# Attention loop of a transformer block: bias adds of the residual rows, the three parts of the normalisation, and the start of the output projection moved to other steps

## The chip, the core and the metric

The kernel runs on one core of a Trainium2 chip. A core has a matrix engine (PE), a vector engine (DVE), an activation engine (ACT), a general engine (POOL) and a queue for transfers (SP); each takes its instructions strictly in the order in which the program issues them, and waits on semaphores for the others. POOL issues transfers too. The metric is the device time of one launch in microseconds (us).

## The reference

One block: attention with low-rank updates on its four projections, a residual sum, a layer normalisation, then a mixture of experts with a shared expert, a residual sum and a second layer normalisation. All data is float32; x is 2 x 1024 x 512, 16 heads of 32.

```python
def lora_linear(x, W, b, Bm, Am):
    out = jnp.einsum('bld,od->blo', x, W) + b
    upd = jnp.einsum('blr,or->blo', jnp.einsum('bld,rd->blr', x, Bm), Am)
    return out + SCALING * upd
...
scores = jnp.einsum('bhqd,bhkd->bhqk', q, k) * SCALE
attn = jax.nn.softmax(scores, axis=-1)
out = jnp.einsum('bhqk,bhkd->bhqd', attn, v)
...
x = _layernorm(x + attention(x), axis=-1)
x = _layernorm(x + moe(x), axis=-1)
```

## The kernel before, in words

The change lies in the attention loop (lines 617 to 855); the projections ahead of it and the experts behind it are as they were.

The work of attention is cut into 16 units (`NU`): a unit is one group of four heads, of one batch, against 512 query rows. Eight groups with two query halves each make the 16. A unit is cut into eight steps, one for each block of 128 keys, so there are 128 steps (`NS`), t = 0 to 127; unit u is t // 8 and step k of it is t % 8. The texts call them "unit 13, step 3". Each step has four slots, one for each head.

A step (`st_step`, line 629) issues for each of its four heads one matmul of transposed scores into a PSUM bank (`st`, line 638) and one exponential on ACT into half of a tile `pt` (line 647). The banks for `st` come from a pool of three (`one`). After the exponential of slot q the functions in `between[q]` are issued, so their place in that list is their place in the order of every engine. Around the steps stand these:

- `maxima`: the scores of a unit are computed twice. The first time, 12 steps ahead (`LEAD`), only the row maxima are wanted: `s1_step` (line 196) does a matmul into one of four banks `s1` (line 203) and a maximum on DVE (line 211). `S_AT` says how many come in each slot, 32 in a unit. After the last of a unit, `finish_max` (line 219) transposes the maxima on PE (into a bank of `one`), splits them into a high and a low part on ACT and DVE (`mh`, `ml`, lines 224 and 225) and sends them by DMA into two extra rows of the query tile, so that the second computation of the scores subtracts them. The last unit's is issued by the loop itself.
- `av_step`: every second step, in slot 3, eight groups of matmuls of the probabilities with the values (line 657).
- `adds` (line 673): the softmax's sums are first added up over key blocks. In a usual unit POOL issues two accumulating transfers after step 2 and two after step 3 (`pt` onto `pt`, line 682), and then eight adds of 128x1024 (line 685), two after each of steps 4 to 7.
- `finish` (line 692): the matmuls with ones that end the sums (line 698), in slot 1 of step 4 of the next unit, a copy on ACT, and a round trip through memory that spreads the 2048 sums over 128 partitions; `invert` (line 719) takes their reciprocals on DVE in step 6 and sends them back as `rb`.
- `normalize` (line 732), in three parts, two units after the unit it belongs to: part 0 multiplies the attention output by the reciprocals (DVE, line 738), part 1 casts the result to its high part (ACT, line 743), part 2 subtracts for the low part (DVE, line 745). Table `NRM` gives for each part (units later, step, slot).
- `load_res` and `add_res` (lines 747 and 752): the 16 blocks of 128 residual rows are loaded into `x1a` and `x1b` at the steps of `RES_AT`, and POOL adds the output projection's bias to them at the steps of `RES_ADDS`, one instruction of 128x512 each.
- `oproj` (line 759): the output projection of one block of rows, 12 matmuls; for the first batch eight blocks, at the steps of `OPROJ_AT`, four matmuls in each of slots 0 to 2. Behind each come, on DVE, the sum with the residual row and the statistics, one step later two small instructions on POOL (`norm_root`) and four steps later the scaling on ACT. It reads what `normalize` left for units 0 to 7.

Within a slot the order is: the maxima that come first, `av_step`, `finish`, the maxima that come second, `adds`, the parts of `normalize`, `invert`, `add_res`, and the projection. The order is written out by hand with these tables; nothing reorders it (`manual_schedule` for all five engines).

In the kernel before, parts 0 and 1 are issued in slot 0 of step 3 and part 2 in slot 2 of step 3. The bias adds stand in steps 9, 13, 25, 29, 41, 45, 57, 61, 73, 77, 89, 93, 103, 105, 114 and 115: up to step 93 that is steps 1 and 5 of the odd units.

Of the kernel before, what the change touches and what calls it, by code (L numbers as in the profile page):

```python
# [20 lines left out]
NU = 16  # L21
# [11 lines left out]
LEAD = 12  # L33
LATE, OP_ONE = (0,), 0
NS = NU * 8
# [19 lines left out]
AVQ = 3  # L55
# [2 lines left out]
FIN = {None: (1, 4, 1), NU - 3: (1, 3, 1), NU - 2: (1, 2, 3)}  # L58
REC = {None: (1, 6, 3), NU - 3: (1, 5, 1)}
NRM = {  # L60
    None: ((2, 3, 0), (2, 3, 0), (2, 3, 2)),
    NU - 3: ((1, 7, 3), (1, 7, 3), (1, 7, 3)),
    NU - 2: ((1, 4, 1), (1, 4, 1), (1, 4, 1)),
}
# [13 lines left out]
    NU - 2: {1: "bb1 dd01", 3: "dd23 vv4", 4: "vv5", 5: "vv6", 6: "vv3 vv7"},  # L78
    NU - 1: {1: "bb1 dd01", 3: "dd23 vv4", 4: "vv5", 6: "vv3"},
}  # L80
OPROJ_AT = (68, 70, 72, 74, 76, 78, 80, 82)
RES_AT = tuple(8 * i + (2 if i % 2 else 6) for i in range(8)) + (70, 74, 86, 90, 100, 102, 106, 110)
RES_ADDS = tuple(t + 3 for t in RES_AT[:14]) + (114, 115)
RB = 2
BTB = 4
AHEAD = 5
# [26 lines left out]
def kernel(  # L113
# [5 lines left out]
    def f(ap):  # L119
        return ap.bitcast(F32)  # L120
# [42 lines left out]
    def load_k(g, cs=slice(0, 1024), hs=slice(0, 4)):  # L163
        kt = Ks[g % 2]
        for blk, hl in ((0, 0), (1, 1), (2, 0)):
            sp.dma_start(
                out=f(kt[32 * blk : 32 * blk + 32, hs, cs]),
                in_=qk_d[1, g // NG, g % NG, hl].rearrange("(h p) t -> p h t", p=32)[:, hs, cs],
            )

    def load_v(g):
        if g < NG:
            vts[g] = x1b[:, :, g * P : g * P + P]
        else:
            vts[g] = mp_.tile([P, 8, P], F32, name=f"vt{g}", tag="vt", bufs=2)
        sp.dma_start(
            out=vts[g],
            in_=v_d[g // NG].rearrange("(c p) d -> p c d", p=P)[
                :, :, (g % NG) * P : (g % NG) * P + P
            ],  # L180
        )

    def load_q(u, hs=slice(0, 4)):
        g, qb = u // 2, u % 2
        for blk, hl in ((0, 0), (1, 0), (2, 1)):
            sp.dma_start(
                out=f(Qs[u % 3][32 * blk : 32 * blk + 32, hs]),
                in_=qk_d[0, g // NG, g % NG, hl].rearrange("(h p) t -> p h t", p=32)[
                    :, hs, qb * 512 : qb * 512 + 512
                ],  # L190
            )
# [27 lines left out]
    def finish_max(u):  # L219
        mp = one.tile([P, 512], F32, name=f"mp{u}", tag="one")  # L220
        pe.transpose(mp[0:16, 0:P], mts[u], ident)
        mh = mp_.tile([16, P], F32R, name=f"mh{u}", tag="mh", bufs=2)
        ml = mp_.tile([16, P], F32R, name=f"ml{u}", tag="ml", bufs=2)
        act.copy(mh, mp[0:16, 0:P])
        dve.tensor_tensor(ml, mp[0:16, 0:P], f(mh), ALU.subtract)
        for i, m_ in enumerate((mh, ml)):
            sp.dma_start(
                out=f(Qs[u % 3][96 + i : 97 + i, :, :]).rearrange(
                    "o h (q t) -> o (h q) t", t=P
                ),  # L230
                in_=f(m_),
            )
# [386 lines left out]
    with ph2, tc.manual_schedule(engines={mybir.EngineType.PE}):  # L619
# [31 lines left out]
        def av_step(t):  # L651
            u, kc = t // 8, t % 8
            g = u // 2
            if kc == 0:
                avs[u] = avp.tile([P, 512], F32, name=f"av{u}", tag="av")
            for h in range(4):
                pe.matmul(  # L657
                    avs[u][32 * h : 32 * h + 32, :],
                    vts[g][:, kc, 32 * h : 32 * h + 32],
                    pts[t, h // 2][:, h % 2, :],  # L660
                    start=kc == 0,
                    stop=kc == 7,
                    skip_group_check=True,
                )
# [4 lines left out]
        def av_out(u):  # L669
            raws[u] = ap.tile([P, 512], F32, name=f"ae{u}", tag="ae", bufs=2)  # L670
            act.copy(raws[u], avs[u])
# [20 lines left out]
        def finish(u):  # L692
            sm = one.tile([P, 512], F32, name=f"sm{u}", tag="one")
            parts = [lambda h, k_=k_: pts[u * 8 + k_, h // 2][:, h % 2, :] for k_ in direct(u)]
            parts.append(lambda h: accs[u, h // 2][:, h % 2, :])
            for i, pf in enumerate(parts):
                for h in range(4):
                    pe.matmul(
                        sm[32 * h : 32 * h + 32, :],
                        ones32,  # L700
                        pf(h),
                        start=i == 0,
                        stop=i == len(parts) - 1,
                        skip_group_check=True,
                    )
            if u >= RDIR:
                rc = ap.tile([P, 512], F32, name=f"rc{u}", tag="rc", bufs=1)
                dve.reciprocal(rc, sm)
                fin[u] = rc
                return  # L710
            rc = ap.tile([P, 512], F32, name=f"rc{u}", tag="rc", bufs=1)
            act.copy(rc, sm)
            sd = dram.tile([4, 512], F32, name=f"sd{u}")
            sp.dma_start(out=sd, in_=rc[0:P:32, :])
            r16 = ap.tile([P, 16], F32, name=f"r16_{u}", tag="r16", bufs=1)
            sp.dma_start(out=r16, in_=sd.rearrange("h (j c) -> (h j) c", c=16))
            fin[u] = r16
# [29 lines left out]
        def load_res(n):  # L747
            b, i = divmod(n, 8)
            r0 = b * L + i * P
            sp.dma_start(out=x1[b][:, i, 0:D], in_=x[r0 : r0 + P, :])  # L750

        def add_res(n):
            b, i = divmod(n, 8)
            pool.tensor_tensor(x1[b][:, i, 0:D], x1[b][:, i, 0:D], bo_bc, ALU.add)
# [29 lines left out]
        def run(gen):  # L784
            for _ in gen:
                pass
# [12 lines left out]
        def at_step(table, t, q):  # L799
            for v in range(max(t // 8 - 2, 0), t // 8):  # L800
                at = table.get(v, table[None])
                at = at[q] if isinstance(at[0], tuple) else at
                if (v + at[0]) * 8 + at[1] == t:
                    yield v

        for t in range(NS):
            u, k = t // 8, t % 8
            if k == 0:

                if u % 2 == 0 and 2 <= u and u // 2 + 1 < B * NG:  # L810
                    for hs in (slice(0, 2), slice(2, 4)):
                        load_k(u // 2 + 1, hs=hs)
                        load_q(u + 2, hs)
                elif u >= 1 and u + 2 < NU:
                    load_q(u + 2)
                if u % 2 and NG <= u // 2 + 1 < B * NG:
                    load_v(u // 2 + 1)
            if t in RES_AT:
                load_res(RES_AT.index(t))
            between = [[], [], [], []]  # L820
            for q in range(4):
                between[q] += [maxima] * S_AT[k][q][0]
            if t + LEAD == NS + 1:
                between[0].append(lambda: finish_max(NU - 1))

            if t and t % 2 == 0:
                between[AVQ].append(lambda: (av_step(t - 2), av_step(t - 1)))
                if k == 0:
                    between[AVQ].append(lambda: av_out(u - 1))
            for v in at_step(FIN, t, 0):  # L830
                between[FIN.get(v, FIN[None])[2]].append(lambda v=v: finish(v))
            for q in range(4):
                between[q] += [maxima] * S_AT[k][q][1]
            if t:
                between[AVQ].append(lambda: adds(t - 1))
            for q in range(3):
                for v in at_step(NRM, t, q):
                    between[NRM.get(v, NRM[None])[q][2]].append(lambda v=v, q=q: normalize(v, (q,)))
            for v in at_step(REC, t, 0):
                if v < RDIR:  # L840
                    between[REC.get(v, REC[None])[2]].append(lambda v=v: invert(v))
            if t in RES_ADDS:
                between[3].append(lambda: add_res(RES_ADDS.index(t)))

            if t in OPROJ_AT:
                op0 = oproj(0, OPROJ_AT.index(t), OPER)
                for q in range(3):
                    between[q].append(lambda q=q, op0=op0: run(op0) if q == 2 else next(op0))
            st_step(t, between)
            for _, fn in [x for x in later if x[0] == 0]:  # L850
                fn()
            later[:] = [(n - 1, fn) for n, fn in later if n]
            if t - NS >= OPROJ1:
                next(op10, None)
# [349 lines left out]
    for st, (blk, nb) in enumerate(BLOCKS):  # L1204
        hss = []
        for c in range(6):
# [22 lines left out]
            for v in range(c * nb, c * nb + nb):  # L1229
                bv, cv = blk + v // 6, v % 6  # L1230
                n = (bv - NB + 1) * 6 + cv
# [10 lines left out]
    with tc.manual_schedule(engines=MAN4):  # L1242
        last = None
        for e in range(E):
            nxt = e + 1
            hss = []
            for c in range(6):
# [4 lines left out]
                n = nxt * 6 + c  # L1252
# [113 lines left out]
```

## Time and profile before

| | |
|---|---|
| median of 3 runs | 1041.44 us (1038.62 to 1042.34) |
| the profiled execution's own time | 1041.44 us |
| its span, first to last instruction | 1039.7 us |
| mean granted clock of PE | 0.992 |
| PE, DVE, ACT, POOL busy | 1007.0, 684.1, 527.8, 535.0 us |
| attention loop (first to last `st` matmul) | 156.4 to 592.5 us of the span |
| bias add, line 754 | 16 times, 1087 to 1937 ns |
| part 0, line 738 (on `rb`) | 14 times, 680 to 4325 ns, median 1190 |
| part 2, line 745 | 15 times, 673 to 821 ns |

Times in the profile are from the span's start. A line of the timeline gives start, duration, engine, source line, operation, what is written and read by the program's names, and how many instructions are merged; in brackets stands how long the engine was idle before and who released it. Lines of groups give busy time and mean duration of one, and then the idle time ahead of them. `L754` is line 754 of the kernel.

### The profile page before, as it was taken

To read this page: it belongs to the slowest core of one execution; us is meant where nothing else is said; L and a number is where in the kernel's file an instruction comes from. 1 tells how busy PE (TensorE), PEld (TensorE's weight loads), DVE (VectorE), ACT (ScalarE), POOL (GpSimd) and SP (SyncE) were. 2 spreads that over 40 slices of the span, in tenths; PEclk is the share of its full clock that TensorE was granted. 3 is DMA by queue.
4 is the path that set the end of the run, shared out by engine and by line. 5 is a ranking of instruction groups with operands and counts; after the bars stand their busy time and mean duration, and the time that the engine had idled before them with its cause. 6 is when DMAs were issued, how large, how long until landed. Compare 5 with 4: busy or idle time off the path is not lost. (4 is left out here: it accounts for less than half of the span.)

```text
span 1039.7 us, 15687 instructions
## 1 busy us (share of the span) xinstructions
PE 1007.0 (97%) x5606; PEld 728.0 (70%) x5606; DVE 684.1 (66%) x1156; ACT 527.8 (51%) x1000; POOL 535.0 (51%) x404
## 2 busy tenths in 40 slices
PE   8999999999999999999989999999999999999994
PEld 6888885555545555655544489888787899999994
DVE  6743788788888887788878773232253467777752
ACT  5322216666767665576657835122122366555662
POOL 5000005989898977869887164000015055666774
PEclk9999999999999999999989999999999999999998
DMA  9866875586868784667964631000009567777621
GB/s 277 289 230 214 245 222 114 126 190 138 190 134 194 154 193 95 127 138 151 197 153 85 151 112 62 22 21 11 31 30 302 177 205 233 258 244 254 222 82 61
DMA packets 87374, 164.75 MB, mean 158 GB/s; under 512 B 15944, under 2 KB 24648, under 8 KB 87296
## 3 DMA queue, kind: packets, MB, share of 16 engines
q1 hardware_dynamic: 74240, 117.59, 38.9%
q0 software_dynamic: 13056, 46.16, 19.9%
q8 instruction: 44, 0.72, 0.3%
q14 instruction: 34, 0.28, 0.1%
HBM read 96.10 MB, written 33.80 MB: 125 GB/s over the span
## 5 line engine op out<-in xcount | busy, mean ns | idle before, releaser
L211 DVE TENSOR_REDUCE mt<-s 128x1 f32<-128x512 f32 x512 | 317.8, 680 | 69.1 <-PE s L203 68.8
L647 ACT ACTIVATE pt<-st 128x512 f32<-128x512 f32 x512 | 266.6, 611 | 113.7 <-PE st L638 107.1
L685 POOL TENSOR_TENSOR pt<-pt,pt 128x1024 f32<-128x1024 f32 x112 | 264.3, 2389 | 37.1 <-ACT pt L647 18.6
L638 PE MATMUL st<-qs,ks 98*128 98x512 f32 x512 | 197.7, 417 | 11.1 <-ACT pt L647 8.8
L203 PE MATMUL s<-ks,qs 96*128 96x512 f32 x512 | 186.8, 403 | 0.2
L638 PEld LDWEIGHTS st<-qs,ks 98*128 98x128 f32 x512 | 92.8, 189 | 94.5 <-ACT pt L647 37.9
L682 POOL DMA_DIRECT2D pt<-pt x64 | 56.2, 1004 | 185.6 <-issue 144.6
L931 PE MATMUL h<-xthe,w13s 128*128 128x256 f32 x704 | 130.0, 283 | 0.0
L203 PEld LDWEIGHTS s<-ks,qs 96*128 96x128 f32 x512 | 97.3, 190 | 36.2 <-DVE mt L211 10.8
L931 PEld LDWEIGHTS h<-xthe,w13s 128*128 128x128 f32 x704 | 110.7, 191 | 0.4
L919 POOL TENSOR_TENSOR w2s<-w2r,w2s 128x512 fp32r<-128x512 f32 x42 | 65.9, 1590 | 68.2 <-ACT w2s L918 65.3
L931 PE MATMUL h<-xtle,w13s 128*128 128x256 f32 x352 | 100.3, 285 | 0.4 <-DVE xtle L484 0.4
L1121 POOL DMA_INDIRECT xd_d<-x1a,slot_i x8 | 7.9, 984 | 139.3 <-DVE slot_i L1118 137.2
L931 PEld LDWEIGHTS h<-xtle,w13s 128*128 128x128 f32 x352 | 67.4, 191 | 1.5 <-DVE xtle L484 0.8
L657 PE MATMUL av<-pt,vt 128*32 128x512 f32 x512 | 62.3, 598 | 0.0
L657 PE MATMUL av<-pt,x1b 128*32 128x512 f32 x512 | 61.6, 598 | 0.0
L1017 PE MATMUL y<-w2s,hs 128*128 128x512 f32 x260 | 60.9, 390 | 0.0
L1017 PEld LDWEIGHTS y<-w2s,hs 128*128 128x128 f32 x260 | 48.2, 188 | 10.2 <-DVE hs L999 0.5
L342 ACT ACTIVATE oh<-o,bqk_sb 128x512 fp32r<-128x512 f32 x32 | 22.0, 690 | 56.2 <-PE o L327 52.5
L586 DVE TENSOR_TENSOR w13s<-x1a,w13s 128x1024 fp32r<-128x1024 f32 x32 | 46.7, 1460 | 4.6 <-issue 4.1
L327 PE MATMUL o<-xh,wh 128*128 128x512 f32 x116 | 45.5, 392 | 1.0 <-DVE ol L343 1.0
L327 PE MATMUL o<-xl,wh 128*128 128x512 f32 x116 | 45.3, 391 | 0.0
(571 smaller groups left out, 1704.2 us busy)
## 6 DMA issues: line engine op xcount, KB each, us to landing
pt<-pt POOLq DMA_DIRECT2D x64, 512.0 KB
x1a<-in_w_dram SPq DMA_DIRECT2D x32, 512.0 KB
w2r<-in_w_dram SPq DMA_DIRECT2D x42, 256.0 KB
ks<-qkd SPq DMA_DIRECT2D x36, 256.0 KB
qkd<-oh SPq DMA_DIRECT2D x32, 256.0 KB
qkd<-ol SPq DMA_DIRECT2D x32, 256.0 KB
qs<-qkd SPq DMA_DIRECT2D x30, 256.0 KB
qs<-qkd SPq DMA_DIRECT2D x36, 128.0 KB
```

What stands on the lines that cost most here:

```text
L203: pe.matmul(s1, Qs[u % 3][0:96, h, qt * P : qt * P + P], Ks[g % 2][0:96, h, kh * 512 : kh * 512 + 512], start=True, stop=True,)
L211: dve.tensor_reduce(mts[u][:, c, kh : kh + 1], s1, AX.X, ALU.max)
L327: pe.matmul(o, lhs, rhs, start=k + i == 0, stop=k + i == KC + 1)
L586: (pool if e < 0 else dve).tensor_tensor(lo, raw, f(hi), ALU.subtract)
L638: pe.matmul(sb, Ks[g % 2][:, h, kc * P : kc * P + P], Qs[u % 3][:, h, :], start=True, stop=True,)
L647: act.activation(pts[t, h // 2][:, h % 2, :], sb, AF.Exp, scale=SCALE)
L657: pe.matmul(avs[u][32 * h : 32 * h + 32, :], vts[g][:, kc, 32 * h : 32 * h + 32], pts[t, h // 2][:, h % 2, :], start=kc == 0, stop=kc == 7 ...
L682: pool.dma_start(out=pts[to, pr], in_=pts[i, pr], accum_op=ALU.add)
L685: eng.tensor_tensor(accs[u, pr], accs[u, pr], pts[i, pr], ALU.add)
L919: pool.tensor_tensor(hl[:, 1, :], raw, f(hl[:, 0, :]), ALU.subtract)
L931: pe.matmul(hp[:, j * 256 : j * 256 + 256], lhs, rhs[:, k, :], start=n == 0, stop=n == 11,)
L1017: pe.matmul(o, lhs, rhs, start=n == 0, stop=n == 16)
```

## The change

Four things are moved; no arithmetic is added or taken away.

- The bias adds go to slot 3 of step 3 of each unit from 1 to 13, one in each and two in unit 13 (steps 11, 19, ..., 107, 107), and the last two stay in steps 114 and 115. The lookup allows two in one step.
- Part 0 of the normalisation goes from slot 0 to slot 1 of step 3, part 1 from slot 0 to slot 3 of step 3, part 2 from slot 2 of step 3 to slot 1 of step 4. The special rows of `NRM` are as before.
- The output projection of the first batch starts in step 70 and ends in step 84, two steps later.
- `finish_max` of the last unit goes from the start of slot 0 in step 117 to slot 3 of step 116, behind `av_step`.

```diff
 NRM = {
-    None: ((2, 3, 0), (2, 3, 0), (2, 3, 2)),
+    None: ((2, 3, 1), (2, 3, 3), (2, 4, 1)),
     NU - 3: ((1, 7, 3), (1, 7, 3), (1, 7, 3)),
     NU - 2: ((1, 4, 1), (1, 4, 1), (1, 4, 1)),
 }
...
-OPROJ_AT = (68, 70, 72, 74, 76, 78, 80, 82)
+OPROJ_AT = (70, 72, 74, 76, 78, 80, 82, 84)
 RES_AT = tuple(8 * i + (2 if i % 2 else 6) for i in range(8)) + (70, 74, 86, 90, 100, 102, 106, 110)
-RES_ADDS = tuple(t + 3 for t in RES_AT[:14]) + (114, 115)
+RES_ADDS = tuple(range(11, 108, 8)) + (107, 114, 115)
...
                 between[q] += [maxima] * S_AT[k][q][0]
-            if t + LEAD == NS + 1:
-                between[0].append(lambda: finish_max(NU - 1))
 
             if t and t % 2 == 0:
                 between[AVQ].append(lambda: (av_step(t - 2), av_step(t - 1)))
                 if k == 0:
                     between[AVQ].append(lambda: av_out(u - 1))
+            if t + LEAD == NS:
+                between[AVQ].append(lambda: finish_max(NU - 1))
...
-            if t in RES_ADDS:
-                between[3].append(lambda: add_res(RES_ADDS.index(t)))
+            for n, at in enumerate(RES_ADDS):
+                if at == t:
+                    between[3].append(lambda n=n: add_res(n))
```

## The prediction

> **What bounds the kernel now.** The page's first part, then the waits of each engine in the attention stretch (150 to 600 us), then the timeline there. Columns of the first line: busy us (share of the span) x instructions.
>
> ```profile
> PE 1007.0 (97%) x5606; PEld 728.0 (70%) x5606; DVE 684.1 (66%) x1156; ACT 527.8 (51%) x1000; POOL 535.0 (51%) x404
> ```
>
> PE is the bound, so only what lets PE issue sooner counts. The change touches the attention loop alone. In its groups (busy us, mean ns of one | idle before, releaser) one row is odd:
>
> ```profile
> L685 POOL TENSOR_TENSOR pt<-pt,pt 128x1024 f32<-128x1024 f32 x112 | 264.3, 2389 | 37.1 <-ACT pt L647 18.6 <-DMA pt<-pt 15.5 <-ACT mh L224 1.2
> L738 DVE TENSOR_TENSOR ae<-ae,rb 128x512 f32<-128x512 f32 x14 | 22.7, 1620 | 0.5 <-DMA rb<-rd 0.4
> L745 DVE TENSOR_TENSOR at_l<-ae,at_h 128x512 fp32r<-128x512 f32 x15 | 10.3, 689 | 0.1
> L754 POOL TENSOR_TENSOR x1a<-x1a,bo_bc 128x512 f32<-128x512 f32 x8 | 9.6, 1194 | 0.0
> ```
>
> L738 (part 0 of the normalisation) and L745 (part 2) are the same work, yet part 0 takes 1620 ns on average. The timeline of unit 13 says why (start us, us, instructions; in brackets the idle time before and its releaser):
>
> ```profile
> 527.47 4.33 DVE L738 TENSOR_TENSOR ae<-ae,rb 128x512 f32<-128x512 f32 x1
> ...
> 528.88 2.37 POOL L754 TENSOR_TENSOR x1b<-x1b,bo_bc 128x512 f32<-128x512 f32 x2
> ...
> 531.15 1.72 POOL L682 DMA_DIRECT2D pt<-pt  x2
> ...
> 531.83 0.62 ACT L743 CAST at_h<-ae 128x512 fp32r<-128x512 f32 x1 [2.25 <-DVE ae L738]
> ...
> 532.99 0.80 PE L638 MATMUL st<-qs,ks 98*128 98x512 f32 x1 [2.63 <-ACT pt L647]
> ```
>
> Part 0 (DVE, to 531.79) ends 0.55 us after the last of POOL's consecutive adds (531.24): DVE stood through the end of L685's add and both L754. ACT's cast (part 1) waits for it ahead of the next exponentials, and PE waits for a score buffer. In unit 3 it is the same on a small scale: part 0 from 241.26 to 243.29, POOL's L754 until 242.74. Where POOL issues DMAs instead (L682), L745 takes 673 to 681 ns.
>
> The wait of 2.63 us also cost clock. The windows show the granted clock at 1.00, then 0.83, 0.50, 0.50, 0.81 (530 to 540 us); shorter waits in units 5 and 11 (1.40 and 1.25) did not.
>
> **How much there is.** From the first score matmul of a step to that of the next, in the timeline: unit 1, which normalises nothing, has 1.97 us in step 3 and 6.68 in step 4, together 8.65. Units 2, 4, 6, 8 (without its projection) and 12 take 9.05; units 3, 5, 7, 11, 13 take 9.55, 10.33, 9.52, 10.20, 14.38. Units 9 and 10 lose 0.22 each in step 3. Over the floor: 5 x 0.40 + (0.90 + 1.68 + 0.87 + 1.55 + 5.73) + 0.44 = 13.2 us. The odd units stand out because the bias adds of steps 1 and 5 fall in odd units only, and that of step 1 is POOL's last work before part 0.
>
> **The change, part by part.**
>
> *Bias adds (POOL, 16 x 1.1 to 1.3 us, as many as before).* They now stand behind the four DMA issues of steps 2 and 3. POOL is free there: it issues four in about 3.5 us (0.87 each) and then waits for the first landing, which lets the next add start 4.55 to 4.67 us after the first issue in units 3, 5, 7, 11 (0.64 us idle in unit 3) and 6.0 to 7.6 in units 2, 4, 6, 8, 12, where key loads are in front. The loads (L750, SP) don't move; each row is loaded at least five steps before its add.
>
> *Part 0, one slot later, behind two score maxima.* DVE reaches it about 2.2 us into step 3 (unit 1: maxima at 1.00 and 1.61). POOL then issues DMAs in every unit, so it takes 0.68. Part 1 goes behind the fourth exponential; the sum's 16 matmuls (1.85 us) cover its 0.61. Gain: the 13.2. Not all stays: exponentials of units 5 and 13 also wait for POOL's last add of the unit before (0.26 and 0.70 us on ACT); with steps shortened I keep 0.3 and 0.6. Units 2 and 12 wait for the landing of the sums (DVE 1.41 and 1.72 us at L722), and starting earlier doesn't bring that forward: 0.8 given back.
>
> *Part 2, step 3 slot 2 to step 4 slot 1.* This is the dangerous one. It leaves POOL's DMA stretch and goes behind the maximum that follows the sum's matmuls. In unit 1 that starts 5.39 us after the start of step 3; with part 0 ahead 5.5, so part 2 comes up at 6.1. In the odd units POOL has by then issued its DMAs (to 3.8 or 4.0), added the bias (to about 5.0) and started the first add of step 4 (5.0 to 7.4); the second follows (7.4 to 9.7). In even units the first add starts 6.56 (unit 8) to 8.46 (unit 12) after step 3, so part 2 is ahead by 0.5 or more: nothing lost.
>
> When does part 2 finish in an odd unit? If DVE gets in between the two adds: 7.4 + 0.55 = 7.95. If only after both: 9.7 + 0.55 = 10.25. PE's next need is the second score matmul of step 5, at 8.65 + 0.25 = 8.9, whose buffer is freed by `ml` (L225), which stands one maximum (0.60) and 0.27 behind part 2: part 2 must end by 8.0. So the stall is 0 or some 2.3 to 2.4 us; the maxima that free PE's `s` banks queue behind part 2 likewise.
>
> Which? In this trace the second add starts late: 0.12 to 0.23 us after the first ends (units 2, 3), because its DMA lands 2.5 us after the first DMA and an add lasts 2.38. With the bias add in front the first add starts up to 0.3 later, and that gap closes. At boundaries without a gap DVE was passed over each time: in units 3, 5, 7, 11 once each and in unit 13 twice. I take "after both" for units 3, 7, 11 (3 x 2.4 = 7.2), "between" for unit 5, where the DMAs start later and the gap stays (1.0, as it ends late), the ends being 0 and 2.4 for each.
>
> The Trainium skill, "SBUF — State Buffer", section "Who interferes with whom", says that a VectorE instruction with two SBUF inputs and a GpSimd one that reads SBUF exclude each other, the first to issue holding the port for one whole instruction. Read so, a waiting DVE would enter at the next boundary: L738 in unit 13 would have taken 2.05 us, not 4.33, and the sum below would be 7.2 us and its clock loss lower. The rows decide against that reading.
>
> Unit 13 has two bias adds in step 3 (steps 103 and 105 become 107). POOL is late there anyway (last add of unit 12 ended 0.97 into step 3): DMAs to 4.9, adds to 7.3, then two adds without gap to 12.0. Part 2 ends at 12.6 against a need of about 8.5: 4.1 lost, plus the clock. Half clock cost this unit 9.36 - 6.80 = 2.56 in step 4; the same again: 6.7.
>
> Clock in units 3, 7, 11: waits of 2.3 us lie between 1.40 (none) and 2.63 (a drop); nearer the upper, so I count a drop in one and a half of three: 3.9, ends 0 and 7.8. The Trainium skill, "TensorE: Matmul & The Clock Gate", section "What's actually happening", puts the return to half rate after an idle window of about 3.4 us; by it these units would lose none of this, but the trace shows a drop with 2.63.
>
> *Last maximum transpose (`finish_max(15)`), one slot earlier.* PE waits 0.82 us at 573.92 for `qs<-ml`. `ml` now stands ahead of DVE's adds of that step (2.36 us) and its DMA goes out some 1.3 us earlier: -0.8; the adds behind it are 0.3 later and have slack (0.4 us idle before the next L738). Ends -0.8 and +0.5.
>
> *Output projection, two steps later.* The same 96 matmuls, still two of eight steps that also carry a sum (68 and 76 become 76 and 84). Behind each row DVE's 0.69 + 0.70 + 0.18 + 0.15, POOL's 0.64 + 0.27 and ACT's 0.82 move along. In units 8 to 10 the steps are 2.8 us longer and POOL idles in them; counted 0. Without that cover, POOL's 8 x 0.9 = 7.2 would queue before the adds.
>
> **Sum**, against the profiled execution's own 1041.44 us (span 1039.7), which is also the median: -13.2 + 0.9 + 0.8 + 7.2 + 1.0 + 6.7 + 3.9 - 0.8 = +6.5, so 1048 us.
>
> **Rivals.**
> 1. *DVE enters between the two adds in all of units 3, 5, 7, 11.* For: the gap of 0.12 to 0.23 us today. Against: the bias add eats it. -13.2 + 0.9 + 0.8 - 0.8 + 1.6 + 6.7 = -4.0: 1037.
> 2. *It enters in unit 13 too*, ending about 10.4 instead of 12.6, without the clock drop (2.0 for 6.7): -8.7: 1033, faster, decided by whether a waiting DVE wins a boundary where POOL's next add is ready.
> 3. *Even units lose too*, if their first add starts before 6.1: five times 2.4 and half a clock drop (1.3), +18: 1066. Against: their landing follows the key loads, which don't move.
>
> **Numbers.** Forecast 0.45, own range 1043 to 1053; rival 1: 0.28; rival 2: 0.17; rival 3: 0.10. A measurement of this kernel tells some 0.5% (5.2 us) from no change. Faster by more: rival 2 and a third of rival 1, 0.27. Slower by more: rival 3 and most of the forecast, 0.43. Range 1032 to 1057, from rival 2 to the forecast with every clock drop.
>
> **What would show it.** L738 at 680 to 700 in all units: step right. L745's mean far over 689, its long ones (3 to 6 us) in odd units ending 0.55 after an L685 add: forecast. L745 at about 2 us there: rival 1. Granted clock below 1.00 in the slices of units 3 to 13: the clock term. No wait for `qs<-ml` near 574: the transpose. Wrong altogether if L745 isn't held at all, or if POOL's adds fall so late that exponentials wait for their `pt` buffers.

## The result, and the profile after

The changed kernel takes 1042.95 us (median of 22 runs, 1041.64 to 1044.21); the kernel before, on the same chip, 1039.80 us (22 runs, 1036.17 to 1043.12). The ratio is 1.0033, 95% interval 1.0023 to 1.0044: slower by 0.33%, some 3.4 us. The direction is that of the forecast, the size half of it, and 0.33% lies below the half per cent that the prediction took as its bound for "no change".

The profiled execution of the changed kernel took 1042.95 us, with a span of 1041.2. First the page's first part (busy us, share of the span, instructions), then the groups of the attention stretch, 150 to 610 us:

```profile
PE 1010.9 (97%) x5606; PEld 727.4 (70%) x5606; DVE 688.0 (66%) x1156; ACT 531.7 (51%) x1000; POOL 538.0 (52%) x404
```

```profile
L685 POOL TENSOR_TENSOR pt<-pt,pt 128x1024 f32<-128x1024 f32 x112 | 266.6, 2420 | 21.2 <-ACT pt L647 10.8 <-DMA pt<-pt 8.4 <-ACT mh L224 1.2
L745 DVE TENSOR_TENSOR at_l<-ae,at_h 128x512 fp32r<-128x512 f32 x15 | 27.5, 1836 | 0.1
L754 POOL TENSOR_TENSOR x1a<-x1a,bo_bc 128x512 f32<-128x512 f32 x8 | 14.7, 1838 | 0.0
L738 DVE TENSOR_TENSOR ae<-ae,rb 128x512 f32<-128x512 f32 x14 | 10.3, 735 | 0.0
```

Parts 0 and 2 have changed places. Part 0 (L738) fell from 22.7 to 10.3 us in all; part 2 (L745) rose from 10.3 to 27.5. POOL's adds (L685) take nearly what they took, 2420 for 2389 ns on average. (L754 is recorded longer because its record now begins while the transfer ahead of it is still being issued: in unit 3 the issue is recorded until 244.52 and the bias add from 243.87.)

The long L745 of unit 13, in the timeline of that unit:

```profile
530.49 2.86 POOL L754 TENSOR_TENSOR x1b<-x1b,bo_bc 128x512 f32<-128x512 f32 x2
532.79 7.47 POOL L685 TENSOR_TENSOR pt<-pt,pt 128x1024 f32<-128x1024 f32 x3
532.88 7.94 DVE L745 TENSOR_TENSOR at_l<-ae,at_h 128x512 fp32r<-128x512 f32 x1
541.48 1.58 PE L203 MATMUL s<-ks,qs 96*128 96x512 f32 x2 [5.21 <-DVE mt L211]
...
545.12 7.07 POOL L685 TENSOR_TENSOR pt<-pt,pt 128x1024 f32<-128x1024 f32 x3 [4.86 <-ACT pt L647]
```

DVE stands from 532.88 to 540.82, through the end of the second bias add and three adds of L685, and ends 0.56 us after the third has ended (540.26). POOL paused there because its fourth add waited for exponentials (4.86 us, the last line), and these for PE, which the waiting DVE held up. The maxima behind part 2 (L211) free PE's `s` banks, so PE waits 5.21 us. What that cost in clock shows in the windows (us; then PE, PEld, DVE, ACT, POOL busy and number, granted clock, DMA share, GB/s):

```profile
538.50:541.00 2.50, 0.00 (x0) 0.00 (x0) 2.50 (x2) 0.00 (x0) 1.76 (x1) 0.88 0.25 44
541.00:543.50 2.50, 2.02 (x4) 1.33 (x5) 2.50 (x6) 0.00 (x0) 0.00 (x0) 0.50 0.10 9
543.50:546.00 2.50, 2.50 (x7) 1.92 (x7) 2.50 (x5) 1.79 (x3) 0.89 (x1) 0.50 0.34 99
```

PE gets half clock while it catches up: 541.00 to 546.00 in these rows.

Unit 3 stands for the odd units without a second bias add. Its timeline:

```profile
243.87 1.95 POOL L754 TENSOR_TENSOR x1a<-x1a,bo_bc 128x512 f32<-128x512 f32 x1
245.65 2.51 POOL L685 TENSOR_TENSOR pt<-pt,pt 128x1024 f32<-128x1024 f32 x1
...
248.22 5.08 POOL L685 TENSOR_TENSOR pt<-pt,pt 128x1024 f32<-128x1024 f32 x2
```

```profile
246.37 2.34 DVE L745 TENSOR_TENSOR at_l<-ae,at_h 128x512 fp32r<-128x512 f32 x1
250.16 0.50 PE L203 MATMUL s<-ks,qs 96*128 96x512 f32 x1 [0.19 <-DVE mt L211]
```

Here DVE comes in after one add: that add ends at 248.16, L745 at 248.72. The second add's record begins at 248.22, 0.06 us after the first has ended. It could not begin sooner, since it waits for its transfer, whose landing the trace puts at 248.08. In unit 13 that transfer had landed at 534.58, 1.09 us before the add ahead of it ended (535.67), so POOL did not pause.

The units by the timeline, from the first score matmul of one to that of the next (us):

| unit | 2 | 3 | 5 | 7 | 8 to 10 | 11 | 12 | 13 | 14 | 0 to 14 |
|---|---|---|---|---|---|---|---|---|---|---|
| before | 25.86 | 26.91 | 27.13 | 26.35 | 101.18 | 27.03 | 25.87 | 31.74 | 24.03 | 417.48 |
| after | 25.45 | 27.21 | 26.97 | 26.85 | 101.02 | 27.83 | 25.47 | 34.64 | 25.85 | 421.86 |

The loop's units 0 to 14 are 4.4 us longer. The stretches before and behind, where the two kernels issue the same work, were 2.9 us shorter in this execution (156.43 to 155.33 and 465.82 to 464.03), so the two profiled executions differ by only 1.5.

### The profile page after: what moved, and what is told of

Same layout as the page of the kernel before. It is cut to its first block, busy times and chain, and to the rows that moved or that the text cites. A ratio compares the mean times of both kernels' runs of the same rounds, so it can differ in the third digit from the quotient of the medians.

```text
span 1041.2 us, 15685 instructions
## 1 busy us (share of the span) xinstructions
PE 1010.9 (97%) x5606; PEld 727.4 (70%) x5606; DVE 688.0 (66%) x1156; ACT 531.7 (51%) x1000; POOL 538.0 (52%) x404
## 5 line engine op out<-in xcount | busy, mean ns | idle before, releaser
L211 DVE TENSOR_REDUCE mt<-s 128x1 f32<-128x512 f32 x512 | 318.3, 680 | 68.8 <-PE s L203 68.6
L647 ACT ACTIVATE pt<-st 128x512 f32<-128x512 f32 x512 | 269.6, 609 | 122.1 <-PE st L638 115.0
L685 POOL TENSOR_TENSOR pt<-pt,pt 128x1024 f32<-128x1024 f32 x112 | 266.6, 2420 | 21.2 <-ACT pt L647 10.8
L203 PE MATMUL s<-ks,qs 96*128 96x512 f32 x512 | 193.0, 413 | 6.5 <-DVE mt L211 6.0
L580 ACT CAST w13s<-x1a 128x1024 fp32r<-128x1024 f32 x32 | 33.4, 1045 | 24.7 <-DMA x1a<-in_w_dram 18.5
```

The lines of the kernel that those rows point to most:

```text
L203: pe.matmul(s1, Qs[u % 3][0:96, h, qt * P : qt * P + P], Ks[g % 2][0:96, h, kh * 512 : kh * 512 + 512], start=True, stop=True,)
L211: dve.tensor_reduce(mts[u][:, c, kh : kh + 1], s1, AX.X, ALU.max)
L647: act.activation(pts[t, h // 2][:, h % 2, :], sb, AF.Exp, scale=SCALE)
L685: eng.tensor_tensor(accs[u, pr], accs[u, pr], pts[i, pr], ALU.add)
```

## The experiments

**My theory after the result:** the bias adds in step 3 and part 2 in step 4 are each good or harmless alone, and only together put a DVE instruction that needs POOL to stand still right behind a bias add, inside POOL's adds. Rivals: moving the parts is what costs, whatever POOL does; the change to the output projection costs; unit 13 alone, with its two bias adds, decides.

### The bias adds alone

```diff
-RES_ADDS = tuple(t + 3 for t in RES_AT[:14]) + (114, 115)
+RES_ADDS = tuple(range(11, 108, 8)) + (107, 114, 115)
```

(on the kernel before, with the lookup that allows two in one step)

> Bias adds in step 3 as in the change; normalisation, projection and last transpose as before. Theory (the loss is part 2 standing behind POOL's adds): part 2 stays in POOL's DMA stretch, so L745 at 0.68 in every unit; L738 no longer has a bias add in front and is at most 1.2 us; units 3, 5, 7, 11, 13 fall to the length of the even ones: 0.5 + 1.3 + 0.5 + 1.2 + 5.3, so 8 to 9 us faster than before (ratio 0.991 to 0.993). Rival (the bias adds in step 3 hold up POOL's own adds and through them the loop): slower than before by 2 us or more.

Measured: 1030.86 us, ratio 0.9903 (0.9870 to 0.9937). The groups of its attention stretch:

```profile
L738 DVE TENSOR_TENSOR ae<-ae,rb 128x512 f32<-128x512 f32 x14 | 12.9, 921 | 0.7 <-DMA rb<-rd 0.6
L745 DVE TENSOR_TENSOR at_l<-ae,at_h 128x512 fp32r<-128x512 f32 x15 | 10.4, 692 | 0.1
```

The whole gained a little more than expected. Part 2 is short in every unit of the loop's general row; part 0 is short too but for units 3, 5 and 13, where it still takes 1.68, 1.65 and 2.04 us behind POOL's last add, more than the 1.2 expected. Unit 13, in the timeline:

```profile
526.86 1.83 POOL L682 DMA_DIRECT2D pt<-pt  x2 [0.34 <-ACT pt L647]
527.14 0.68 DVE L745 TENSOR_TENSOR at_l<-ae,at_h 128x512 fp32r<-128x512 f32 x1
528.39 2.65 POOL L754 TENSOR_TENSOR x1b<-x1b,bo_bc 128x512 f32<-128x512 f32 x2
530.69 5.02 POOL L685 TENSOR_TENSOR pt<-pt,pt 128x1024 f32<-128x1024 f32 x2
```

Part 2 ran while POOL issued transfers, and the same two bias adds and the same L685 stand behind it, with nobody waiting for POOL. Unit 13 takes 26.77 us, against 31.74 before and 34.64 after. This one line of the change gives 1%.

### The three parts and the projection alone

```diff
-    None: ((2, 3, 0), (2, 3, 0), (2, 3, 2)),
+    None: ((2, 3, 1), (2, 3, 3), (2, 4, 1)),
...
-OPROJ_AT = (68, 70, 72, 74, 76, 78, 80, 82)
+OPROJ_AT = (70, 72, 74, 76, 78, 80, 82, 84)
```

> The three parts of the normalisation and the projection as in the change, bias adds and last transpose as before. Theory: L738 0.68 everywhere; L745 some 2.3 us in units 3, 5, 7, 11, which stay 0.3 shorter to 0.8 longer than before; unit 13 has its bias adds ahead of the DMAs again, its first add lands later than part 2, so L745 is 0.7 there and the unit loses its 7 us: 2 to 5 us faster than before (ratio 0.995 to 0.998). Rival (bias adds are the cause): 9 us faster or more, with no long L745.

Measured: 1035.61 us, ratio 0.9948 (0.9928 to 0.9968): faster too. Its unit 13:

```profile
527.24 2.38 POOL L754 TENSOR_TENSOR x1b<-x1b,bo_bc 128x512 f32<-128x512 f32 x2
529.51 3.50 POOL L682 DMA_DIRECT2D pt<-pt  x4
533.30 0.68 DVE L745 TENSOR_TENSOR at_l<-ae,at_h 128x512 fp32r<-128x512 f32 x1
534.17 2.37 POOL L685 TENSOR_TENSOR pt<-pt,pt 128x1024 f32<-128x1024 f32 x1 [1.15 <-DMA pt<-pt]
```

With no bias add behind the transfers POOL waits 1.15 us for the landing, and part 2 fits into that wait. In units 3, 7 and 11 it doesn't (2450, 2587 and 2897 ns), and these take 27.62, 27.49 and 27.83 us. So the moved parts cost in three units at least what they cost in the changed kernel (27.21, 26.85 and 27.83), and unit 14 takes 26.85 instead of 24.03; still the whole is faster, because unit 13 takes 27.18. Moving the parts has a price, but by itself it doesn't make the kernel slower: as the cause of the slowdown the first rival falls. Apart, the two edits give 1.0% and 0.5%; together, with the transpose (no more than 0.4% by its own run below), they lose 0.3%.

### The second bias add of unit 13 elsewhere

```diff
-RES_ADDS = tuple(range(11, 108, 8)) + (107, 114, 115)
+RES_ADDS = tuple(range(11, 108, 8)) + (113, 114, 115)
```

(on the changed kernel)

> The change with the second bias add of step 107 moved to step 113. Theory: in unit 13 L745 falls from 7.9 to 2.3 to 3 us, PE's wait of 5.2 us and the half clock behind it go, the unit is 8 us shorter (34.6 to some 27): 4 to 5 us faster than before (ratio 0.995 to 0.997). Rival (unit 13's loss is POOL being late from unit 12, not the second bias add): L745 stays over 5 us, ratio 1.002 to 1.004.

Measured: 1035.94 us, ratio 0.9961 (0.9941 to 0.9981). The group of part 2:

```profile
L745 DVE TENSOR_TENSOR at_l<-ae,at_h 128x512 fp32r<-128x512 f32 x15 | 22.0, 1464 | 0.1
```

Against the changed kernel's 1.0033 this is 0.7% less, some 7.5 us. Part 2 of unit 13 takes 2319 ns instead of 7942, and unit 13 takes 27.44 us instead of 34.64, which is nearly all of it. The sign of the whole change thus hangs on one instruction of about 1.2 us on POOL, an engine with a busy share of 52%: with it DVE finds no gap between POOL's instructions until three adds later; without it DVE finds one after the first add. So the third rival is right about the sign, but unit 13 is not all: with the parts in their old places (below) the same bias adds give 0.9904 instead of 0.9961. Units 0 to 14 are 6.6 us longer here than there, 3.0 of them in unit 14 and 1.2 and 2.0 in units 3 and 11.

### The projection alone, the transpose alone

```diff
-OPROJ_AT = (68, 70, 72, 74, 76, 78, 80, 82)
+OPROJ_AT = (70, 72, 74, 76, 78, 80, 82, 84)
```

> The kernel before with the output projection from step 70, all else as before. Theory: the 2.8 us of a step with projection leave unit 8 and come to unit 10, nothing else changes: within 1 us of before, ratio 0.998 to 1.002. Rival (the later projection has a price of its own, in unit 11 whose bank maxima wait behind a row's statistics): 1 to 3 us slower, ratio 1.001 to 1.003.

Measured: 1044.42 us, ratio 1.0014 (0.9988 to 1.0040); units 8 to 10 take 100.45 us. By the time alone a price of 0.4% is not excluded, which would be the whole slowdown; but units 8 to 11, in which its work lies, are no longer than before: without steps 3 and 4 of unit 11, where part 0's stall varies, they take 117.96 us together against 118.01. The second rival falls by the units, not by the time.

```diff
-            if t + LEAD == NS + 1:
-                between[0].append(lambda: finish_max(NU - 1))
...
+            if t + LEAD == NS:
+                between[AVQ].append(lambda: finish_max(NU - 1))
```

> The kernel before with the last maximum transpose in step 116 as in the change, all else as before. Theory: only units 14 and 15 change; PE's wait of 0.82 us for the rows of maxima at the start of unit 15 goes, nothing else moves: 0 to 1 us faster than before, ratio 0.998 to 1.001. Rival (the loss of the change in unit 14 is this part): unit 14 gets 2 us longer, ratio 1.001 to 1.003.

Measured: 1039.15 us, ratio 0.9986 (0.9964 to 1.0008), too little to be told from nothing by the time. The units tell more: unit 14 takes 22.84 instead of 24.03 and step 0 of unit 15 takes 3.30 instead of 2.95, so 0.85 us are gained, and the wait for `qs<-ml` is gone. In its profiled execution unit 3 took 28.57 and unit 5 29.09 us, against 26.91 and 27.13 in that of the kernel before, with the same instructions in the same order there. How long part 0 stands in the odd units of the kernel before thus varies from one execution to the next: summed as in the prediction, steps 3 and 4 lie 16.5 us over the floor in this execution, against 13.2.

### Unit 12's parts as before

In the changed kernel unit 14 had become longer by 1.8 us, of which the prediction said nothing. Its timeline:

```profile
562.39 2.98 POOL L754 TENSOR_TENSOR x1b<-x1b,bo_bc 128x512 f32<-128x512 f32 x2
564.50 1.43 DVE L738 TENSOR_TENSOR ae<-ae,rb 128x512 f32<-128x512 f32 x1
566.59 0.50 PE L638 MATMUL st<-qs,ks 98*128 98x512 f32 x1 [1.31 <-DVE mt L211]
568.33 3.29 PE L657 MATMUL av<-pt,vt 128*32 128x512 f32 x16
```

Unit 14 normalises unit 12. There the bias adds stay in steps 114 and 115, and part 0 in slot 1 instead of slot 0 now meets them: 1.43 us for 0.68. PE waits 1.31 us, and 16 matmuls that take 1.92 us elsewhere take 3.29, as the granted clock falls (0.64 from 567.0 to 569.5). The experiment gives unit 12 its old places within the changed kernel:

```diff
     None: ((2, 3, 1), (2, 3, 3), (2, 4, 1)),
+    NU - 4: ((2, 3, 0), (2, 3, 0), (2, 3, 2)),
```

> The change, but the three parts for unit 12, which are issued in unit 14, stand where they stood before. Theory: in the change part 0 comes up in unit 14 behind the sum's matmuls and a bias add (L738 1.43 us), PE then waits 1.3 us for a bank and gets a half-clock stretch; with the old places L738 is 0.7, the wait and the half clock go, unit 14 falls from 25.9 to some 24 us: 2 us faster than the change, ratio to before 1.000 to 1.003. Rival (the transpose in step 116 is what unit 14 pays for): unit 14 stays at 25.5 or more.

Measured: 1041.48 us, ratio 1.0015 (1.0000 to 1.0029). In its unit 14 (line numbers are one higher):

```profile
560.87 0.68 DVE L739 TENSOR_TENSOR ae<-ae,rb 128x512 f32<-128x512 f32 x1
```

Unit 14 takes 22.85 us, 3.0 less than in the changed kernel and the same as with the transpose alone. By the time the gain is 0.2%, with intervals that overlap (1.0000 to 1.0029 and 1.0023 to 1.0044), so it is the unit that shows it. The new places of unit 12's parts cost 3.0 us there and hide the transpose's gain. The edit moves all three back; part 0 is the only one of them that is held in the changed kernel (part 2 takes 681 ns there).

### Part 2 right behind the bias add

If a waiting DVE instruction is held by POOL's adds, it should be held in every unit when it is issued at the time of the bias add:

```diff
-    None: ((2, 3, 1), (2, 3, 3), (2, 4, 1)),
+    None: ((2, 3, 1), (2, 3, 3), (2, 3, 3)),
```

(on the changed kernel)

> The change with part 2 in slot 3 of step 3, right behind part 1, instead of step 4 slot 1. Theory: part 2 comes up some 4.0 us into step 3, while POOL runs the bias add (3.5 to 5.2), and waits for its end in every unit: L745 some 1.7 us in even units too, ending 0.55 us after L754; the maxima behind it are late by 1 to 2 us and even units get 0.5 to 1.5 us longer (26 to 27 instead of 25.5); unit 13, with two bias adds, stays the worst. Ratio to before 1.003 to 1.012. Rival (only POOL's long adds of step 4 hold DVE, a bias add doesn't): L745 0.68 in even units, ratio 0.988 to 0.994.

Measured: 1061.62 us, ratio 1.0212 (1.0179 to 1.0244), the mechanism as expected, its price nearly twice the upper end. Unit 2, an even one, which lost nothing in the changed kernel:

```profile
217.39 1.76 POOL L754 TENSOR_TENSOR x1a<-x1a,bo_bc 128x512 f32<-128x512 f32 x1
217.88 1.83 DVE L745 TENSOR_TENSOR at_l<-ae,at_h 128x512 fp32r<-128x512 f32 x1
220.55 2.37 POOL L685 TENSOR_TENSOR pt<-pt,pt 128x1024 f32<-128x1024 f32 x1 [1.40 <-DMA pt<-pt]
```

Part 2 waits for the bias add (to 219.15) and ends 0.56 behind it. Behind it stand the last maxima of the unit, which PE's transpose (L221) needs. The waits of PE, 150 to 600 us (in total, times, longest):

```profile
PE mp L221 <- DVE mx L214: 25.9, 11, 5.1
```

In this one run both outcomes are seen behind the same bias add, in unit 3 and in unit 7:

```profile
244.58 1.95 POOL L754 TENSOR_TENSOR x1a<-x1a,bo_bc 128x512 f32<-128x512 f32 x1
245.07 4.31 DVE L745 TENSOR_TENSOR at_l<-ae,at_h 128x512 fp32r<-128x512 f32 x1
246.36 2.46 POOL L685 TENSOR_TENSOR pt<-pt,pt 128x1024 f32<-128x1024 f32 x1
...
364.44 1.95 POOL L754 TENSOR_TENSOR x1a<-x1a,bo_bc 128x512 f32<-128x512 f32 x1
364.92 2.03 DVE L745 TENSOR_TENSOR at_l<-ae,at_h 128x512 fp32r<-128x512 f32 x1
366.44 2.72 POOL L685 TENSOR_TENSOR pt<-pt,pt 128x1024 f32<-128x1024 f32 x1
```

In units 3 and 5 the next add's record begins 0.17 and 0.15 us *before* L754 has ended, and L745 is passed over and stands through that add as well (4312 and 4327 ns). In unit 7 it begins 0.05 us *after* L754 has ended, and L745 goes in (2027 ns). Units 9 and 10 are an exception: there POOL's next instruction is a power of 128x1 (L609), recorded from 0.81 us before L754 has ended, and L745 goes in all the same:

```profile
427.37 2.05 POOL L754 TENSOR_TENSOR x1b<-x1b,bo_bc 128x512 f32<-128x512 f32 x1
427.92 2.06 DVE L745 TENSOR_TENSOR at_l<-ae,at_h 128x512 fp32r<-128x512 f32 x1
428.61 1.77 POOL L609 TENSOR_TENSOR sca<-sca,expo 128x1 f32<-128x1 f32 x1
```

### The bias adds in steps 5 and 6

```diff
-RES_ADDS = tuple(t + 3 for t in RES_AT[:14]) + (114, 115)
+RES_ADDS = tuple(8 * u + k for u in range(1, 14, 2) for k in (5, 6)) + (114, 115)
```

(on the kernel before: still two in each odd unit, but none ahead of part 0)

> The kernel before with the bias adds moved to steps 5 and 6 of the odd units (before: steps 1 and 5), all else as before. Theory (before lost its time to the bias add of step 1 alone): L738 at most 1.2 us in all units, odd units as long as even ones, unit 13 at full clock: 8 to 9 us faster than before (ratio 0.991 to 0.993). Rival (POOL is the bound in odd units wherever its adds stand): within 2 us of before.

Measured: 1038.31 us, ratio 0.9972 (0.9942 to 1.0001): the expectation of the time was missed, and its ten runs lie far apart (1032.46 to 1042.30). The profiled execution is one of the shortest (1033.14 us, by itself a gain of the size expected); what follows is read from it, and no trace shows what the long ones do. The odd units are freed as expected (25.87 to 25.91 us, unit 13 25.91), but the even units now take 26.71 to 26.73, with L738 at 2419 ns: two bias adds late in the odd unit make POOL late at the start of the next, and its last add there meets part 0. In this execution the stall has moved on by one unit.

### What beats both

The bias adds and the transpose, without the moved parts and projection:

> Bias adds in step 3 and the last transpose in step 116 as in the change; the parts of the normalisation and the projection as before. Theory: the gain of the bias adds alone (ratio 0.990) and up to 1 us more: ratio 0.988 to 0.991. Rival: the two don't add up, 0.991 to 0.994.

Measured: 1029.36 us (1028.50 to 1029.88), ratio 0.9904 (0.9877 to 0.9932). Units 0 to 14 take 407.56 us, against 417.48 before. With the second bias add of unit 13 in step 113 as well:

```diff
-RES_ADDS = tuple(t + 3 for t in RES_AT[:14]) + (114, 115)
+RES_ADDS = tuple(range(11, 108, 8)) + (113, 114, 115)
```

> Bias adds in step 3, but the second one of step 107 in step 113, and the last transpose in step 116; parts and projection as before. Theory: with part 2 inside POOL's DMA stretch the second bias add of unit 13 stood in nobody's way, so this is within 1 us of the bias adds and the transpose without that move: ratio 0.988 to 0.992. Rival (two bias adds in one unit cost wherever part 2 stands): 0.984 to 0.988.

Measured: 1032.72 us, ratio 0.9902 (0.9865 to 0.9938), units 0 to 14 407.47 us: no difference that can be told (the two ran on different chips, so the ratios are to be compared). Where part 2 is done before the bias adds begin, the second one costs nothing. That is the counter-proof to the run with that add moved in the changed kernel.

Last, all three parts in slot 0 of step 3, with part 1 on DVE too, so that nothing has to pass between engines:

```diff
-    None: ((2, 3, 0), (2, 3, 0), (2, 3, 2)),
+    None: ((2, 3, 0), (2, 3, 0), (2, 3, 0)),
...
-NRM_DVE = (NU - 3, NU - 2)
+NRM_DVE = tuple(range(NU - 1))
```

(on the kernel with one bias add a unit and the transpose)

> As the run with one bias add a unit, but part 1 on DVE (0.43 us in units 14 and 15 before) and all three parts in slot 0 of step 3. Theory: what is left over the floor of 8.65 us in steps 3 and 4 (0.40 in even units) is ACT's cast between the exponentials; without it steps 3 and 4 come to 8.65 to 8.75 in even units and the kernel is 2 to 4 us faster than with the cast on ACT: ratio 0.984 to 0.988. Rival (DVE is then the one that is late, since three instructions stand ahead of the maxima): no faster, 0.990 or more.

Measured: 1033.91 us, ratio 0.9903 (0.9863 to 0.9942): a miss, no faster. The even units came out as expected (steps 3 and 4 8.70 us, units 25.5), but in units 3, 5 and 13 part 0 still takes 1.13, 2.06 and 1.98 us behind POOL's last add, now with two more instructions ahead of the maxima; their step 4 takes 7.17, 7.84 and 7.84 us instead of 6.7. In unit 10 it takes 7.29, though part 0 isn't held there; why is open.

## Why the prediction was right or wrong

| term of the sum | predicted, us | measured, us |
|---|---|---|
| part 0 no longer held | -13.2 | -13.2 |
| units 5 and 13 still wait for POOL | +0.9 | +0.6 (steps 3 and 4 at 8.99 and 8.93, floor 8.65) |
| sums' landing, units 2 and 12 | +0.8 | 0 (they became 0.41 and 0.40 shorter) |
| part 2 in units 3, 7, 11 and 5 | +7.2 +1.0 | +4.9 (1.10 +1.10 +1.65 +1.06, over the floors of steps 5 and 6) |
| part 2 in units 9 and 10 | 0 | +1.3 |
| part 2 in unit 13, clock included | +6.7 | +8.3 (7.06 in step 5, 1.22 in step 6) |
| clock in units 3, 7, 11 | +3.9 | 0 |
| transpose, with unit 14 | -0.8 | +1.8 (gain of 1.2 in unit 14, part 0 there 3.0) |
| sum | +6.5 | +3.7 |

The measured terms make 3.7 of the 4.4 us by which units 0 to 14 grew; of the 0.7 left, 0.5 stand in step 0 of units 3, 5, 7 and 13 (0.08 to 0.26 each), and their cause is open.

That the sum came out at half the forecast, and not further off, is partly luck. The terms for units 3, 5, 7 and 11 and their clock were 7.2 us too high; unit 13, units 9 and 10 and unit 14, too low or left out, made up 5.5 of that.

**Part 0: right.** L738 takes 681 or 682 ns in all of units 2 to 13, and steps 3 and 4 of the units without POOL's lateness are at 8.65, the floor taken from unit 1. The size -13.2 belongs to one execution of the kernel before; in the run with the transpose alone the same stalls came to 16.5. That the small terms behind it were right in one case and nothing in the other matters little.

**Part 2 in units 3, 5, 7 and 11: wrong, the step that decided the size.** The prediction said that "the first add starts up to 0.3 later, and that gap closes", and took "after both" for units 3, 7, 11. In the trace the gap shrank and did not close: the second add's record begins 0.06, 0.05, 0.05 and 0.09 us after the first has ended, in units 3, 5, 7 and 11, and DVE goes in there every time (L745 2342, 2326, 2343 and 2900 ns, each ending 0.55 to 0.56 after the first add). It is rival 1's branch. The first add was not delayed as far as reckoned: in unit 3 its transfer landed at 245.51, its record begins at 245.65, and the bias add ended at 245.82, so it lost at most 0.17 us, not 0.3. The second transfer landed 2.57 us after the first, and its add's record begins 0.13 us after that landing, when the first add was over. The run with part 2 right behind the bias add shows the other outcome where the records overlap by 0.15 and 0.17. Rival 1 was reckoned with 1.6 for four units; they cost 4.9. About half of the difference is step 6, 0.4 longer in each, with DVE's maxima late behind part 2; the rest is step 5 itself, 0.7 longer in three of them and 1.25 in unit 11, instead of 0.4.

**Clock in units 3, 7, 11: wrong with it.** No wait of PE in these units is longer than 0.3 us from step 3 on, and the granted clock doesn't fall.

**Unit 13: right in kind, too small.** The prediction had part 2 ending at 12.6 into step 3, behind two adds; it stood through three, the third of which lasted another 2.3 us (537.97 to 540.26). That one was ready since two exponentials of step 5 were already done (537.15), so POOL had no reason to pause; the fourth had to wait for the next two. The wait of PE came to 5.21 us rather than 4.1, and half clock from 540.41 to 547.24 came with it.

**Units 9 and 10: not seen.** The prediction costed part 2 only where no projection runs; POOL's first add runs there too when part 2 comes up, and part 2 takes 2207 and 2011 ns.

**Transpose: right; unit 14: not seen.** The gain is there by itself (0.85). What I passed over is that the general row of the table also serves unit 12, and that the bias adds of steps 114 and 115 lie around the place where part 0 now falls. The two runs above show it by 3.0 us.

**Rivals.** Rival 2 (DVE enters in unit 13 too) falls: it was passed over at three boundaries. Rival 3 falls: L745 takes 680 or 681 ns in units 2, 4, 6, 8, 12. The lapse common to the errors: I reckoned starts from sums of durations, good to some 0.1 or 0.2 us, where a gap of 0.05 (unit 7 after) and an overlap of 0.03 (unit 7 before) give different outcomes.

**On the port rule.** The Trainium skill, "SBUF — State Buffer", section "Who interferes with whom", gives the port that the two engines share to whoever issues first, for the whole instruction. Taken as one instruction at a time, the case agrees only where POOL pauses: in unit 3 a pause of 0.06 us is enough. In unit 13 DVE was held for 7.94 us through four instructions of POOL, which one instruction at a time doesn't give.

## What to carry to other kernels

When two engines can't run at once, place the short instruction where the other engine does something else (here: POOL issuing DMAs), rather than between its long instructions: in a gap-free run of those it waits for the whole run, and the maxima queued behind it take PE with them. Two edits that move toward the same few microseconds must be priced together: here they gave 1.0% and 0.5% apart and lost 0.3% together. And a table's general row serves units whose surroundings differ, so each unit must be looked at, the last ones above all.

## What the runs showed of the hardware

- Whether a held DVE instruction gets in between two of POOL's adds (L685, L754) follows from whether the second one's record begins before the first has ended. In all boundaries between such adds that these runs hold, a start 0.03 us or more after the end let DVE in (the least, 0.03, in unit 7 of the run with one bias add in unit 13; 0.05 to 0.09 in the changed kernel); overlaps passed it over, those of 0.03 to 0.07 us in units 3, 5, 7, 11 and 13 of the kernel before as well as those of 0.53 to 0.56 in unit 13 after. The prediction's own rows thus held the test; what it lacked was that so small a gap is enough. It is not a rule for all of POOL's instructions: the power of 128x1 let DVE in with an overlap of 0.81. Where DVE got in after a gap below 0.1 us, POOL's next add was recorded 2.7 us long instead of 2.4, so it then waited in turn. How the choice is made, the traces don't show.
- Every L738 and L745 that POOL's adds held ended 0.54 to 0.56 us after the last of these adds had ended.
- The clock falls after waits shorter than I had thought: 1.31 us (unit 14 of the changed kernel) and 1.58 (unit 5 with the transpose alone) were followed by half clock, 1.40 and 1.25 in the kernel before were not, nor was 1.82 in unit 11 of the run with part 2 right behind the bias add. So length alone doesn't decide it here. The half-clock stretches in the attention loop measured 3.41 or 6.83 us. The Trainium skill, "TensorE: Matmul & The Clock Gate", section "What's actually happening", speaks of an idle window of about 3.4 us; no run here shows that a wait must be that long, and 1.31 was enough.
